# Compressed keys by four TensorE products over rows read back from memory, and later rows' statistics tied to program order

## The chip, the cores and the metric

One core of a Trainium2 chip runs the whole program: one launch, float32 throughout apart from small index products. The metric is device time in microseconds (us) of that core, the median of a few executions. Smaller is better. Engines are named as in the profile: PE is TensorE (matrix products and transposes), DVE is VectorE, ACT is ScalarE, POOL is GpSimd, SP is SyncE, which here only issues DMAs. PE writes to PSUM banks, which DVE or ACT must read out before a bank can be written again.

## The reference

Two transformer layers on four sequences of 512 tokens, 512 wide. Each layer adds an attention and a mixture of experts to its input. The part that matters here is the first layer's attention on the layer-normed rows `xn`. Besides a local window it attends to compressed entries, each a softmax-weighted sum of 4 neighbouring tokens:

```python
w_log = (hidden_states @ Wcmp + bcmp).reshape(Bq, C, RATIO)      # C = 128 entries, RATIO = 4
w_cmp = jax.nn.softmax(w_log, axis=-1)
entries = jnp.einsum('bcr,bcrh->bch', w_cmp, hidden_states.reshape(Bq, C, RATIO, HID))
ck = apply_rope(rmsnorm(entries @ Wk + bk, kn_w), block_ends)
cv = entries @ Wv + bv
sc = jnp.einsum('bhsd,bcd->bhsc', q, ck) * scale                 # scores against entries, top 8 kept
```

## The kernel before

**Rows and steps.** The 2048 tokens are 16 row tiles of 128 (n = 0..15), four to a sequence b. The first layer's attention has 16 heads in 8 groups g of two; a step is one pair (g, b), and there are 32, in the order of `steps` (g outer, b inner). Each step computes scores, context and output of its own pair and, in between, the projections of the next step (`project`: seven block products p1 to p7, each of two chunks and two contraction halves, line 661). Everything this change touches lies before step 4, in the first tenth of the run: row statistics, compression, and steps 0 to 3.

**Row tiles.** `layernorm(n)` (line 215) takes the statistics on DVE (`bn_stats` 221, aggregate 223, add 224), the inverse root on POOL (225, 227), the normed row `xn` (DVE for the first four tiles, ACT at 234 for the others: that is what `scaled` means), stores it to `xnd` in device memory (237), transposes it on PE (242) and copies the transpose into `xnT` on ACT (243). `start_sequence(n)` does all of it for one tile. Tiles 4 to 7 are called between the parts of the first projection, ahead of the loop; 8 to 11 in step 0 and 12 to 15 in step 1, one at each of the places (i, 0) to (i, 3) of `run0`.

**Logits and compression.** `first_logits(b)` computes the compression and router logits of a sequence from its four transposed tiles (252: four products of 32 columns of weights against 512 columns, then 259 to turn them back). `compress(b)` is a generator of four parts; for b = 0 they run ahead of the loop, for b = 1, 2, 3 at places 0, 1, 3.5 and 4 of step b - 1. Part 1 turns the logits (584) and takes the softmax on DVE and ACT (586 to 593); then four DVE operations spread each of the four weight columns over an identity (596). Part 2 lets one PE product with a matrix of ones put all 512 weights on every partition (`wB`, 599), and for each of the four chunks of 128 features DVE multiplies the transposed rows by them (603) and sums groups of four (604). Part 3 projects the entries (`kv`, 609), adds biases (611, 613), and norms and rotates `ck` (564 to 566, 573 to 576, 616). Part 4 transposes `ck` (619) into `ckT` (620), which the scores of step b need at line 744.

**Order.** The code's order is not the order on the engines: a scheduler of the tile framework places the instructions of all engines when the program is built, by its own estimates, and each engine then runs its list in order. `tc.keep_in_program_order(x)` ties an instruction to its place in the code, behind what the code issues on that engine before it. Before, this is done in `layernorm` only for the first four tiles, so that statistics of later tiles may move ahead. DVE's temporaries of `layernorm` are in a pool of three buffers, which limits how far ahead.

**PSUM.** Eight banks: three for projections and outputs ("mm"), three for scores, context, logits, `wB` and `kv` ("sc"), two for transposes ("tr"). A tag's banks are taken in turn.

## Time and profile before

| | us |
|---|---|
| median of 3 executions | 2073.09 (2073.08 to 2075.61) |
| the profiled execution's own time | 2074.66 |
| its span in the profile | 2072.6 |
| first score product of step 0 starts (line 744) | 61.44 |
| of step 1 | 102.89 |
| of step 2 | 149.12 |
| of step 3 | 193.31 |

Times in the profile are from the span's start. The step starts frame the stage the change is in: steps 0, 1 and 2 take 41.5, 46.2 and 44.2 us. In the profile's lines `L661` is a line of the kernel, an arrow points from a tile's operand to its result, `x4` counts instructions of the machine, and a bracket gives the idle time before an instruction and the engine that ended it. One float32 product of the code is two such PE instructions, so one block product and chunk of `project` is four of 384 columns (1.29 us where they run one behind the other) and a transpose of 128 by 128 is one.

### The profile page before, as it was taken

Reading aid. Unit: us, or ns where it says so; the run is one execution under the profiler, and the core shown is the slowest. Engines: PE = TensorE matmul, PEld = TensorE weight load, DVE = VectorE, ACT = ScalarE, POOL = GpSimd, SP = SyncE. Lnnn points to the kernel's source line nnn. Section 1 sums busy time; section 2 is a strip of 40 time slices with the busy share of each in tenths; the row PEclk is TensorE's granted clock in tenths of the full one; section 3 lists DMA queues with packets and bytes.
Section 4 is the critical chain, followed back from the end, with each engine's and each line's share of the span. In section 5 each row is a group of like instructions: output and inputs, shape, how many; then the busy total and the mean of one; then the engine's idle time right before and its main releaser. Section 6 shows DMA issues by size and latency. Waiting matters only on the chain.

```text
span 2072.6 us, 27984 instructions
## 1 busy us (share of the span) xinstructions
PE 2017.7 (97%) x9130; PEld 1205.3 (58%) x9130; DVE 1452.0 (70%) x3543; ACT 867.9 (42%) x2600; POOL 754.3 (36%) x761
## 2 busy tenths in 40 slices
PE   6999999999999999999999999999999999999997
PEld 4666666666666666666666666666334445445442
DVE  7888967666766666676667778787596555557775
ACT  4554444444444443444444455454243432333332
POOL 4422244443423333344333444353114332332550
PEclk9999999999999999999999999999999999999999
DMA  7102133333333343234443222121317765773551
GB/s 250 68 31 62 42 118 120 143 108 103 130 130 104 109 155 103 92 135 166 183 170 116 70 76 85 42 72 62 119 51 244 263 243 196 257 243 123 158 163 52
DMA packets 98906, 267.23 MB, mean 129 GB/s; under 512 B 14400, under 2 KB 27840, under 8 KB 87488
## 3 DMA queue, kind: packets, MB, share of 16 engines
q0 software_dynamic: 27072, 148.91, 21.4%
q1 hardware_dynamic: 70528, 114.34, 16.4%
q10 hardware_dynamic: 1152, 2.10, 0.3%
q8 instruction: 75, 1.23, 0.2%
q14 instruction: 79, 0.65, 0.1%
HBM read 222.05 MB, written 42.73 MB: 128 GB/s over the span
## 4 chain that ended last, share of the span: by engine, by line
PE 81%; DVE 8%; ACT 3%; POOL 2%; DMA 2%; issue 1%; SPq 0%; ACTq 0%; POOLq 0%; DVEq 0%
PE p L661 23%; PE hp_r L518 12%; PE op L828 10%; PE st L753 4%; PE st L1224 3%; PE qp L1200 3%; PE sp L744 3%; PE cx L1238 2%; PE ca L797 2%; PE o L1307 2%; PE trm_r L506 2%; PE vp L1160 1%; PE trq L681 1%; PE trk L687 1%; PE cc L800 1%
## 5 line engine op out<-in xcount | busy, mean ns | idle before, releaser
L828 PE MATMUL op<-Wo,cT 128*128 128x512 f32 x512 | 230.6, 598 | 5.3 <-DVE lv L725 2.9
L518 PE MATMUL hp_r<-we_r,xT_r 128*128 128x512 f32 (+1 forms) x592 | 224.8, 596 | 0.0
L470 POOL DMA_INDIRECT xr_r<-xnd,rows_r x72 | 89.4, 1242 | 331.6 <-PE trm_r L506 298.2
L761 POOL TENSOR_TENSOR lT<-lT,lmask 128x512 f32<-128x512 f32 (+1 forms) x128 | 157.6, 1244 | 140.8 <-ACT lT L757 140.6
L661 PE MATMUL p<-wT,x 128*128 128x384 f32 x512 | 179.6, 493 | 0.5 <-DVE wT L119 0.5
L661 PE MATMUL p<-wB,x 128*128 128x384 f32 x512 | 175.9, 488 | 4.0 <-DVE u L717 4.0
L661 PE MATMUL p<-wA,xnT 128*128 128x384 f32 x512 | 174.0, 492 | 0.2 <-DVE u L696 0.2
L828 PEld LDWEIGHTS op<-Wo,cT 128*128 128x128 f32 x512 | 92.0, 190 | 115.0 <-issue 77.2
L564 ACT ACTIVATE sq<-qb 128x128 f32<-128x128 f32 x384 | 118.9, 310 | 93.0 <-DVE qb L710 44.9
L1226 ACT ACTIVATE pT<-st 128x1024 f32<-128x1024 f32 x128 | 123.7, 1014 | 62.7 <-PE st L1224 57.0
L518 PEld LDWEIGHTS hp_r<-we_r,xT_r 128*128 128x128 f32 (+1 forms) x592 | 83.8, 170 | 97.3 <-issue 91.8
L831 DVE TENSOR_TENSOR acc<-acc,op 128x512 f32<-128x512 f32 x128 | 87.4, 685 | 69.4 <-PE op L828 69.0
L661 PEld LDWEIGHTS p<-wB,x 128*128 128x128 f32 x512 | 93.9, 190 | 68.5 <-issue 10.2
L661 PEld LDWEIGHTS p<-wT,x 128*128 128x128 f32 x512 | 94.5, 193 | 63.5 <-issue 6.7
L661 PEld LDWEIGHTS p<-wA,xnT 128*128 128x128 f32 x512 | 95.6, 193 | 61.0 <-issue 2.9
L675 ACT ACTIVATE qb<-qb,ss 128x128 f32<-128x128 f32 x256 | 81.9, 390 | 110.7 <-POOL ss L566 108.6
L508 ACT COPY xT_r<-trm_r 128x512 f32<-128x512 f32 x72 | 41.8, 581 | 198.0 <-PE hp_r L518 188.3
L757 ACT ACTIVATE lT<-st,ss 128x256 f32<-128x256 f32 (+1 forms) x128 | 47.2, 449 | 175.4 <-PE st L753 175.3
L753 PE MATMUL st<-qkT 128*128 128x256 f32 (+1 forms) x512 | 110.4, 357 | 0.0
L534 POOL DMA_INDIRECT row_r<-yd,slot_r x64 | 74.2, 1160 | 94.0 <-DVE row_r L1341 35.8
L753 PEld LDWEIGHTS st<-qkT 128*128 128x128 f32 x512 | 93.1, 193 | 11.4 <-issue 1.4
L566 POOL TENSOR_TENSOR ss<-ss,nhalf 128x6 f32<-128x6 f32 x64 | 95.7, 1496 | 5.3
(360 smaller groups left out, 4334.2 us busy)
## 6 DMA issues: line engine op xcount, KB each, us to landing
x<-xsd SPq DMA_DIRECT2D x112, 256.0 KB, 3.1
yd<-yr_r SPq DMA_DIRECT2D x72, 256.0 KB, 3.4
wA<-in_wA SPq DMA_DIRECT2D x16, 384.0 KB, 3.6
wB<-in_wB SPq DMA_DIRECT2D x16, 384.0 KB, 7.6
xnd<-xn SPq DMA_DIRECT2D x24, 256.0 KB, 2.0
accd<-acc SPq DMA_DIRECT2D x18, 256.0 KB, 2.0
acc<-in_x SPq DMA_DIRECT2D x16, 256.0 KB, 4.9
Wo<-in_Wo SPq DMA_DIRECT2D x8, 512.0 KB, 3.6
```

What stands on the lines that cost most here:

```text
L470: G.indirect_dma_start(out=out, out_offset=None, in_=src, in_offset=at_rows(idx))
L518: PE.matmul(hp[ts(h, m), :], lhsT=xT[:, k, ts(h, m)], rhs=w[:, ts(k, HID)], start=(k == 0), stop=(k == KC - 1))
L534: G.indirect_dma_start(out=x, out_offset=None, in_=self.yd, in_offset=at_rows(self.r.slot[:, k, n : n + 1]))
L564: A.activation(sq, x[:, h, :], AF.Square, accum_out=ss[:, h : h + 1])
L566: G.tensor_tensor(ss, ss, nhalf[:, 0:n], ALU.pow)
L661: PE.matmul(p, lhsT=x[:, k, ts(c, P)], rhs=w[:, k, :], start=(k == 0), stop=(k == 1))
L675: A.activation(x[:, j, :], x[:, j, :], AF.Copy, scale=sq[t][:, j : j + 1])
L753: PE.matmul(st[:, ds((t % 2) * 256, n)], lhsT=qkT[:, HG + h, ts(t, P)], rhs=qkT[:, h, ds(t * P, n)], start=True, stop=True)
L761: G.tensor_tensor(dst, dst, lmask.rearrange("p a w j -> p (a w j)")[:, 0:n], ALU.mult)
L828: PE.matmul(op, lhsT=cT[:, h, ts(t, P)], rhs=wo[:, h, :], start=(h == 0), stop=(h == HG - 1))
L831: V.tensor_tensor(acc[:, n, :], acc[:, n, :], op, ALU.add)
L1226: A.activation(pt[:, ts(pair, 2), :], st, AF.Exp, scale=SCALE1)
```

## The change

Line numbers on the minus side are those of the profile. In `compress`, the rows of a sequence are read back from `xnd` in one DMA of 1 MB at the start of part 1, queued on SP. A matrix `fold` (the sum of the identity's four blocks of 32 columns, so that fold[p, j] = 1 where p modulo 32 is j) is made once on POOL. DVE scales 32 columns instead of 128 by each weight column; PE transposes the result and ACT copies it (`wsel`); four products, each with 32 columns of `wsel` as weights and one row tile of 512 features as the moving side, give all 128 entries in one bank; ACT copies them, four transposes turn them, and ACT copies them into `entT`. From `kv` on nothing is different. The multiplications and sums at 603 and 604, and `wB`, are gone. In `layernorm`, tiles 4 to 15 of the first layer's sequence are now tied to program order as the first four were, and in `scores` the first DVE operation of head 0 is tied in steps with i < 2.

```diff
--- before.py
+++ after.py
@@ -175,8 +175,13 @@
 
     ident = const.tile([P, P], F32, tag="ident", name="ident")
     make_identity(nc, ident)
+
+    fold = sp0.tile([P, FEW], F32, tag="fold", name="fold", bufs=1)
     nhalf = const.tile([P, 8], F32, tag="nhalf", name="nhalf")
     G.memset(nhalf, -0.5)
+    G.tensor_tensor(fold, ident[:, ts(0, FEW)], ident[:, ts(1, FEW)], ALU.add)
+    for n in (2, 3):
+        G.tensor_tensor(fold, fold, ident[:, ts(n, FEW)], ALU.add)
     A.activation(small.tile([P, 8], F32, tag="warm", name="warm", bufs=1), nhalf, AF.Exp)
     ones_sq = const.tile([P, P], F32, tag="ones_sq", name="ones_sq")
     G.memset(ones_sq, 1.0)
@@ -216,7 +221,7 @@
 
 
 
-        pin = tc.keep_in_program_order if n < TC else (lambda x: x)
+        pin = tc.keep_in_program_order if n < TC or scaled else (lambda x: x)
         st = small.tile([P, 6], F32, tag="st", name=f"st_{n}")
         pin(V.bn_stats(st, acc[:, n, :]))
         mv = small.tile([P, 2], F32, tag="mv", name=f"mv_{n}")
@@ -578,6 +583,8 @@
     def compress(b, pool):
 
         w_row = row_w[b]
+        rows_ = pool.tile([P, TC, HID], F32, tag="rows4", name=f"rows4_{b}", bufs=1)
+        nc.sync.dma_start(out=rows_, in_=xnd[ts(b, S), :].rearrange("(n p) h -> p n h", p=P))
 
         wt = psum("tr", f"wt_{b}")
         for r in range(RATIO):
@@ -591,17 +598,26 @@
         A.activation(w1, w1, AF.Exp, bias=mx, accum_out=sm)
         V.reciprocal(sm, sm)
         V.tensor_scalar(w1, w1, sm, None, ALU.mult)
-        wd = pool.tile([P, C, RATIO], F32, tag="prod", name=f"wd_{b}", bufs=1)
+
+        wd = pool.tile([P, FEW, RATIO], F32, tag="wd", name=f"wd_{b}", bufs=1)
         for r in range(RATIO):
-            V.tensor_scalar(wd[:, :, r], ident, w1[:, r : r + 1], None, ALU.mult)
+            V.tensor_scalar(wd[:, :, r], fold, w1[:, r : r + 1], None, ALU.mult)
         yield
-        wB = psum("sc", f"wB_{b}")
-        PE.matmul(wB, lhsT=ones_sq, rhs=wd.rearrange("p c r -> p (c r)"), start=True, stop=True)
+        tr = psum("tr", f"trw_{b}")
+        PE.transpose(tr[:, 0:P], wd.rearrange("p c r -> p (c r)"), ident)
+        wsel = pool.tile([P, P], F32, tag="wd", name=f"wsel_{b}", bufs=1)
+        A.copy(wsel, tr[:, 0:P])
+
+        ep = psum("sc", f"ent_{b}")
+        for n in range(TC):
+            PE.matmul(ep[ts(n, FEW), :], lhsT=wsel[:, ts(n, FEW)], rhs=rows_[:, n, :], start=True, stop=True)
+        ent = pool.tile([P, HID], F32, tag="lr", name=f"ent_{b}", bufs=1)
+        A.copy(ent, ep)
+        tr = psum("tr", f"tre_{b}")
+        for k in range(KC):
+            PE.transpose(tr[:, ts(k, C)], ent[:, ts(k, P)], ident)
         entT = pool.tile([P, KC, C], F32, tag="entT", name=f"entT_{b}", bufs=1)
-        for k in range(KC):
-            prod = pool.tile([P, C, RATIO], F32, tag="prod", name=f"prod_{b}_{k}", bufs=1)
-            V.tensor_tensor(prod.rearrange("p c r -> p (c r)"), xnT[:, k, ts(b, S)], wB, ALU.mult)
-            V.tensor_reduce(entT[:, k, :], prod, AX.X, ALU.add)
+        A.copy(entT, tr.rearrange("p (k c) -> p k c", k=KC))
         yield
         kv = psum("sc", f"kv_{b}")
         for i, w in enumerate((wk, wv)):
@@ -744,7 +760,9 @@
             PE.matmul(sp[:, seen[t]], lhsT=qkT[:, h, ts(t, P)], rhs=ckT[:, b, 0 : 32 * (t + 1)],
                       start=True, stop=True)
         s = wk0.tile([P, SEEN[TC - 1].stop], F32, tag="s", name=f"s_{nm}")
-        V.tensor_tensor(s, sp[:, 0 : SEEN[TC - 1].stop], cmask, ALU.add)
+        s_ = V.tensor_tensor(s, sp[:, 0 : SEEN[TC - 1].stop], cmask, ALU.add)
+        if i < B - 2 and h == 0:
+            tc.keep_in_program_order(s_)
         lT = wk0.tile([P, TC * 2 * P - P], F32, tag="lT", name=f"lT_{nm}")
         for half in range(2):
             st = psum("sc", f"st{half}_{nm}")
```

The built program's order of instructions differs up to step 3 on PE, DVE, ACT, POOL and SP, and nowhere behind it.

## The prediction

> **What bounds it now.** First the page's busy times, then the stage in windows cut at the last product of each step's output (columns: busy us and instructions of PE, weight loads, DVE, ACT, POOL; granted PE clock; DMA share; GB/s).

> ```profile
> PE 2017.7 (97%) x9130; PEld 1205.3 (58%) x9130; DVE 1452.0 (70%) x3543; ACT 867.9 (42%) x2600; POOL 754.3 (36%) x761
> 55.00:101.90 46.90, 45.38 (x227) 31.91 (x225) 40.09 (x129) 25.38 (x85) 19.30 (x28) 0.96 0.19 69
> 101.90:148.15 46.25, 45.23 (x234) 31.14 (x234) 38.02 (x106) 24.21 (x81) 12.18 (x13) 1.00 0.10 35
> 148.15:192.90 44.75, 43.50 (x216) 29.65 (x216) 38.32 (x107) 20.96 (x76) 11.27 (x13) 1.00 0.22 69
> ```

> PE is full everywhere, in steps 0 to 2 too, where DVE is some 84% busy. So DVE time is worth only the PE idle time that it causes. I get that by adding up what PE has to do, with durations from the chain of waits (start, us, what):

> ```profile
> 60.65 0.33 PE trck L619
> 60.98 0.44 PE trg_r L259 x4
> 61.44 1.25 PE sp L744 x8
> 62.69 2.99 PE st L753 x8
> ...
> 68.69 1.52 PE st L753 x8
> ...
> 70.53 0.44 PE trx L242 x4
> 70.97 0.65 PE p L661 x2
> 71.62 0.86 PE wB L599 x2
> ...
> 101.97 0.99 PE lg_r L252 x8
> ```

> A block product is 4 x 0.32 = 1.29 us, four transposes 0.44, scores 1.09, `kv` 1.76 (16 x 0.11), an output 6.87. Later steps with two experts are 45.8 us apart; less 2 x 3.9 for the experts, 38.0 is a dense step. Sequence work comes on top. Step 1 (102.89 to 149.12) needs 38.0 + 1.8 (row transposes) + 1.0 + 0.4 + 0.4 (logits) + 0.9 (`wB`) + 1.8 + 0.1 = 44.4 of its 46.2: 1.8 lost. Step 2 needs 41.7 of 44.2: 2.5 lost, half of it waiting for `wd` (596). Step 0 needs 39.2 of 41.5, and 1.5 of its loss is the slow `st` above. From 41.04 to 61.44, ahead of step 0, PE needs 16.2 of 20.4: 4.2 lost. All that any relief can give back is 4.2 + 2.3 + 1.8 + 2.5 = 10.8 us.

> **What is removed and added.** Per sequence DVE loses eight operations (603, 604) and most of four:

> ```profile
> 46.61 0.67 DVE L603 TENSOR_TENSOR prod<-xnT,wB 128x512 f32<-128x512 f32 x1
> 47.67 0.67 DVE L604 TENSOR_REDUCE entT<-prod 128x128 f32<-128x512 f32 x1
> ```

> 8 x 0.67 = 5.4, and some 0.5 of the 0.9 to 2.0 that `wd` takes at a quarter of the width: 6 us each, 24 in all. PE loses `wB` (0.86) and gets five transposes (0.55) and four 32-column products like the logits' (0.99): +0.7 each, which lies on the bound engine. ACT gets copies of 128 and twice 512 columns (0.3 + 2 x 0.58): on an engine 45 to 55% busy their length is hidden, but they stand in its queue between PE and its next product. `fold` (three small POOL operations) runs before POOL's first use at 4.69, idle time. SP gets four 1 MB reads. Other 1 MB loads land in 5.4 to 10.1 us; rows 0 to 3 are stored long before, and the read is queued behind the fourth `xsd` store at some 41, so it lands by 46.5 to 51, and PE wants it at 49.9: hidden, or 1 us late. Later ones have more room; what is queued behind them on SP (`wB`, `xsd`) is wanted a step later.

> **What moves.** This decides. Before, statistics of tiles 6 and 7 ran on DVE at 40 to 41, and those of 8 to 11 by 43, far ahead of PE. Tied down, they stand behind what the code issues earlier, and in the new list of PE the transposes `trx` of a tile stand ahead of work that is ready. I merged the new lists by hand, each engine in order, with the durations shown. From statistics to transpose it is:

> ```profile
> 41.04 0.69 DVE L221 BATCH_NORM_STATS2 st<-acc 128x6 f32<-128x512 f32 x1
> 40.09 0.55 POOL L225 TENSOR_TENSOR mv<-mv,nhalf 128x1 f32<-128x1 f32 x1 [1.36 <-DVE mv L223]
> 40.74 0.27 POOL L227 TENSOR_SCALAR mv<-mv 128x1 f32<-128x1 f32 x1
> 43.87 0.80 ACT L234 ACTIVATE xn<-acc,mv 128x512 f32<-128x512 f32 x1
> ```

> *Ahead of step 0.* PE is dense from 41.4 on: eight block products 10.3, the new ones and `trq`, `trx` 2.4, `kv` 1.8, so `kv` ends at 55.9 (57.9 before). Only then can DVE add the biases and rotate `ck`, and behind these tile 7's statistics are tied: 0.5 + 1.0 (two `qb`) + 0.7 + 0.65 + other work in between 1.05 = 3.9, POOL 0.9, ACT 0.8: its `trx` starts at 61.6. PE has 0.44 to do meanwhile (`trk`) and idles 5.2. The copy to `xnT` stands behind two `qb` scalings that wait for a 1.34 us power on POOL: ready at 63.7; logits 1.0; scores start at 64.7 instead of 61.44: **+3.3**, its own share of the added PE work included. Bounds: +1.5 if DVE's in-between work is done earlier, +4.5 if the fetch is late too.

> *Step 0.* Tile 8's statistics follow the spread weights, whose softmax follows head 0's scores: DVE reaches them at 75.9, `trx` can start at 78.3, PE is there at 75.8 with the ready `trs` behind it: 2.5 lost. `wsel` waits in ACT's queue for `xn`, `xnT` and `s`: 0.7. Tile 11 costs about 1.0, and the 0.7 lost before is regained at best: with the 0.7 of PE work, 2.5 + 0.7 + 1.0 - 0.7 + 0.7 = 4.2; as `trs` no longer waits later I take **+3.5**. Bounds 0 (PE so late that rows are ready) and +6.

> *Step 1.* The list puts six block products ahead of tile 12's `trx`. The statistics of 12 and 13 delay the reading of the third (0.7 lost on the bank), `trx` 1.3, `wsel` 0.9, tile 14 0.8, the context's banks 0.7: 4.4 new, 1.8 old gone, 0.7 work: **+3.3**. Bounds -1.1 and +5.

> *Step 2* has no tiles: up to all of 2.5 regained, 0.7 paid: -1.8 to +0.7. By my merge the second context starts 0.3 earlier; I take **-0.5**.

> Sum 3.3 + 3.5 + 3.3 - 0.5 = 9.6. From step 3 on nothing is reordered, and PE is 97% busy, so the shift reaches the end whole. The span becomes 2082.2, and that execution 2084.3 by the 2.06 around its span; on the median of 2073.09 it is **2082.7**.

> [...] The row first (windows; PE busy, then clock):

> ```profile
> 58.00:60.00 2.00, 1.18 (x4) 0.38 (x2) 2.00 (x9) 0.50 (x3) 0.81 (x2) 1.00 0.39 139
> 60.00:62.00 2.00, 1.32 (x10) 1.09 (x11) 2.00 (x6) 1.55 (x8) 0.24 (x1) 1.00 0.34 131
> 62.00:64.00 2.00, 2.00 (x9) 1.73 (x9) 1.54 (x11) 0.21 (x1) 1.92 (x3) 0.59 0.35 131
> ```

> After four us at 60% busy, the clock is 0.59 and `st` takes 2.99 instead of 1.52. I put the same loss into both programs. [...]

> **Rivals.** *A, faster.* DVE's 24 us are what PE's losses come from; DVE runs ahead again, tied rows included, and PE never meets a `trx` too early. For it: before, DVE's chain carries `wd` into `wB` (1.0 and 1.2 idle). Against it: tiles 6 to 15 give up a lead of 10 us or more. Half of the 10.8 us won, and three quarters of the 2.7 of PE work paid, is -3.4; all and all paid, -8.1. It lies between 2065.0 and 2069.7, say 2068. It decides if step 0's scores start before 61.

> *B, no change.* The first gap is as I say (+3.3), but in steps 0 to 2 new waits only replace the old: 2.0 of PE work, -4.3 for the losses of steps 1 and 2, some +1: 2073.1 + 3.3 + 2.0 - 4.3 + 1.0 = 2075.

> *C, slower by the fetch.* SP holds a read until the last of its four tiles is stored (row stores land in 2.0), and tiles are now late; each of the four `ent` waits some 2 us more: 9.6 + 4 x 2 gives 2090. Against it: 2 to 20 us of room for all but the first.

> **Numbers.** Forecast (2077.3 to 2087) 0.58, C and worse 0.08, B 0.18, A 0.16. Since 0.2% (4.1 us, about what can be told from no change here) parts the signs, slower takes the forecast and C, 0.66; same is B, 0.18; faster is A, 0.16. Sum of the lower bounds 1.5 + 0 - 1.1 - 1.8 = -1.4, of the upper +16.2 (2089). Below stands A with 0.16, of which I leave half out: 2068 to 2089.

> **What would show it.** Right: `sp` of step 0 starts near 64.7 behind a PE gap of 4 to 6 us that tile 7's `xn` ends; `trx` waits of 1 to 3 us for `xn` (line 239 of the new code) in steps 0 and 1; DVE some 24 us less busy up to 195. Wrong: no PE wait on `xn` behind 45, or waits on the fetched rows, or step 3's scores starting before 193.

## The result, and the profile after

| | before | changed |
|---|---|---|
| median, us | 2073.51 (2073.08 to 2075.61, 4 runs) | 2093.53 (2092.06 to 2094.98, 4 runs) |
| ratio | | 1.0094, 95% interval 1.0082 to 1.0107 |
| the profiled execution: its own time / its span | 2074.66 / 2072.6 | 2092.06 / 2090.3 |

The changed kernel is slower, by 20.0 us on the medians, where 9.6 were forecast. The two profiled executions are 17.4 apart, because that of before lay 1.2 above its median and that of the changed kernel 1.5 below. What the traces can explain is 17.7 us of span. The starts of the steps' scores say where they arise:

| first score product of | before | changed | later by | forecast |
|---|---|---|---|---|
| step 0 | 61.44 | 65.15 | 3.71 | 3.3 |
| step 1 | 102.89 | 116.83 | 13.94 | 6.8 |
| step 2 | 149.12 | 166.51 | 17.39 | 10.1 |
| step 3 | 193.31 | 211.02 | 17.71 | 9.6 |
| step 4 | 224.88 | 242.60 | 17.72 | 9.6 |

From step 4 to step 23 the difference stays at 17.71 to 17.72. So step 0 grew by 10.2 us where 3.5 were forecast, and everything else came within 0.9.

The first lines of the changed kernel's page answer to those shown before, with the busy times of all engines:

```profile
PE 2024.3 (97%) x9174; PEld 1206.1 (58%) x9174; DVE 1435.2 (69%) x3511; ACT 874.4 (42%) x2612; POOL 755.3 (36%) x764
```

DVE has 16.8 us less to do (24 were forecast), PE is busy for 6.6 longer. The same columns as in the windows of the prediction (busy us and instructions of PE, weight loads, DVE, ACT, POOL; granted PE clock; DMA share; GB/s), first from the end of the first projection to step 0's scores and then step by step, and below that some stretches of 2 us:

```profile
55.80:65.15 9.35, 2.92 (x15) 0.81 (x14) 5.68 (x17) 6.50 (x23) 3.48 (x6) 0.79 0.12 43
65.15:116.83 51.68, 45.93 (x228) 31.52 (x225) 31.27 (x102) 23.56 (x70) 14.71 (x20) 0.91 0.29 101
116.83:166.51 49.68, 47.14 (x245) 30.89 (x241) 34.54 (x109) 26.62 (x86) 16.21 (x21) 1.00 0.18 61
166.51:211.02 44.51, 43.67 (x225) 30.08 (x221) 33.59 (x98) 22.62 (x78) 12.09 (x13) 1.00 0.24 74
...
64.00:66.00 2.00, 2.00 (x12) 0.85 (x5) 1.25 (x2) 0.66 (x2) 0.58 (x1) 0.50 0.60 223
72.00:74.00 2.00, 2.00 (x15) 1.88 (x15) 1.76 (x6) 0.56 (x2) 0.97 (x2) 1.00 0.05 12
82.00:84.00 2.00, 2.00 (x6) 0.93 (x4) 0.65 (x2) 1.23 (x5) 0.00 (x0) 0.50 0.21 77
```

PE is idle for 5.8 of the 51.7 us of step 0, where before it was idle for none, and its clock averages 0.91 there against 0.96. DVE, busy for 86% of step 0 before, is at 61%: the engine that was relieved is not the one that PE waits for. The waits of PE between 41 and 215 us name what it waits for (us in total, times, longest):

```profile
PE trx L247 <- ACT xn L239: 12.6, 7, 4.9
PE lg_r L257 <- ACT xnT L248: 1.5, 1, 1.5
PE trw L607 <- DVE wd L604: 0.8, 1, 0.8
```

It is the normed rows, seven times, and never the fetched rows: `ent` of sequence 0 starts at 49.12 with no wait. PE's list around step 0 shows the two long waits (start, us, what; in brackets the idle time and who ended it):

```profile
55.26 0.60 PE L703 MATMUL trk<-ident,qb 128*128 128x128 f32 x4
60.76 0.79 PE L247 MATMUL trx<-ident,xn 128*128 128x128 f32 x4 [4.90 <-ACT xn L239]
...
63.28 1.94 PE L257 MATMUL lg_r<-xnT,wr 128*32 128x512 f32 x8 [1.53 <-ACT xnT L248]
65.15 2.08 PE L760 MATMUL sp<-ckT,qkT 128*128 128x32 f32 x8
...
74.45 3.39 PE L677 MATMUL p<-wT,x 128*128 128x384 f32 x10
80.91 0.65 PE L247 MATMUL trx<-ident,xn 128*128 128x128 f32 x4 [3.07 <-ACT xn L239]
...
81.81 1.49 PE L677 MATMUL p<-wT,x 128*128 128x384 f32 x2
```

Read the durations too. Scores take 2.08 here and 1.06 a few us later, a pair of 384-column products 1.49 instead of 0.81: after each of the two long gaps the clock is at 0.50, from 61.1 to 71.4 and from 81.6 to 85.0.

Why tile 8's statistics are late is seen in DVE's list, with what POOL does at that time:

```profile
75.40 2.50 DVE L604 TENSOR_SCALAR wd<-fold,w 128x32 f32<-128x32 f32 x4
77.81 0.68 DVE L226 BATCH_NORM_STATS2 st<-acc 128x6 f32<-128x512 f32 x1
...
75.44 2.26 POOL L779 TENSOR_TENSOR lT<-lT,lmask 128x512 f32<-128x512 f32 x2 [2.47 <-ACT lT L775]
```

The statistics stand behind the spread weights, as forecast, and these four operations of 32 columns take 2.50 us beside two POOL operations, where the median of all sixteen is 0.24 each. So the quarter width saved nothing at the place that counts. That POOL is what stretches them is only read from the overlap; no run took it apart.

### The profile page after: what moved, and what is told of

The parts are those of the page before. It is cut to its first block, busy times and chain, and to the rows that moved or that the text cites. A ratio compares the mean times of both kernels' runs of the same rounds, so it can differ in the third digit from the quotient of the medians.

```text
span 2090.3 us, 28075 instructions
## 1 busy us (share of the span) xinstructions
PE 2024.3 (97%) x9174; PEld 1206.1 (58%) x9174; DVE 1435.2 (69%) x3511; ACT 874.4 (42%) x2612; POOL 755.3 (36%) x764
## 3 DMA queue, kind: packets, MB, share of 16 engines
q8 instruction: 76, 1.25, 0.2%
## 4 chain that ended last, share of the span: by engine, by line
PE 76%; DVE 9%; ACT 3%; POOL 2%; issue 2%; DMA 1%; ACTq 0%; DVEq 0%; POOLq 0%
PE p L677 22%; PE hp_r L523 12%; PE op L846 10%; PE st L771 4%; PE st L1242 3%; PE qp L1218 3%; PE sp L760 2%; PE cx L1256 2%; PE o L1325 2%; PE ca L815 2%; PE trm_r L511 2%; PE vp L1178 1%; PE trq L697 1%; PE cb L818 1%; PE ca L813 1%
## 5 line engine op out<-in xcount | busy, mean ns | idle before, releaser
L569 ACT ACTIVATE sq<-qb 128x128 f32<-128x128 f32 x384 | 118.8, 309 | 85.3 <-DVE qb L726 41.7
L849 DVE TENSOR_TENSOR acc<-acc,op 128x512 f32<-128x512 f32 x128 | 87.6, 685 | 71.5 <-PE op L846 71.1
L677 PEld LDWEIGHTS p<-wT,x 128*128 128x128 f32 x512 | 94.9, 194 | 63.5 <-issue 5.8
```

What stands on the lines that cost most here:

```text
L569: A.activation(sq, x[:, h, :], AF.Square, accum_out=ss[:, h : h + 1])
L677: PE.matmul(p, lhsT=x[:, k, ts(c, P)], rhs=w[:, k, :], start=(k == 0), stop=(k == 1))
L849: V.tensor_tensor(acc[:, n, :], acc[:, n, :], op, ALU.add)
```

## The experiments

All profiles in one table. The four columns of steps say how much later than in the kernel before each step's first score product starts, in the profiled execution; the last columns are medians and ratios to the runs of before on the same chip (medians 2073.5 to 2074.0). A start also moves when PE's list puts work on the other side of it; the start of step 3, behind which nothing is reordered, is free of that.

| kernel | step 0 | step 1 | step 2 | step 3 | median, us | ratio, 95% interval |
|---|---|---|---|---|---|---|
| changed | 3.71 | 13.94 | 17.39 | 17.71 | 2093.53 | 1.0094 (1.0082 to 1.0107) |
| comp_alone | -0.22 | 3.08 | 3.80 | 4.12 | 2079.60 | 1.0028 (1.0017 to 1.0040) |
| ties_alone | 6.19 | 13.15 | 18.56 | 18.01 | 2091.77 | 1.0092 (1.0076 to 1.0107) |
| free_4_to_7 | -2.74 | 5.55 | 9.01 | 9.35 | 2086.13 | 1.0060 (1.0046 to 1.0074) |
| tie_4_to_7 | 3.78 | 9.63 | 10.36 | 10.68 | 2085.38 | 1.0064 (1.0050 to 1.0078) |
| no_score_tie | 7.44 | 15.30 | 18.74 | 19.06 | 2096.17 | 1.0110 (1.0095 to 1.0126) |
| filled_gap | 3.08 | 10.91 | 14.36 | 14.68 | 2091.90 | 1.0089 (1.0075 to 1.0102) |
| dve_relief | -5.29 | -2.67 | -2.37 | -1.56 | 2074.48 | 1.0001 (0.9992 to 1.0010) |
| comp_late_part2 | -1.60 | -1.09 | 0.09 | -0.47 | 2076.05 | 1.0011 (1.0001 to 1.0020) |
| comp_wd_on_act | -1.75 | 0.72 | 1.97 | 2.41 | 2078.81 | 1.0025 (1.0014 to 1.0037) |
| before_filled5 | -3.07 | -4.05 | -4.07 | -4.05 | 2070.51 | 0.9987 (0.9977 to 0.9996) |
| before_filled6 | -0.33 | -1.44 | -1.46 | -1.48 | 2072.73 | 0.9997 (0.9988 to 1.0006) |
| comp_late_filled5 | -4.87 | -4.36 | -3.16 | -3.72 | 2073.02 | 1.0004 (0.9995 to 1.0013) |

### The two halves of the change

The compression without the ties:

```diff
-        pin = tc.keep_in_program_order if n < TC or scaled else (lambda x: x)
+        pin = tc.keep_in_program_order if n < TC else (lambda x: x)
...
-        if i < B - 2 and h == 0:
-            tc.keep_in_program_order(s_)
```

> The new compression with all three ties undone (layernorm of tiles 4 to 15 and the score's first DVE operation). Theory P (the ties: statistics stand late in DVE's list and PE's transposes wait for them): no wait of PE on xn above 0.5 us behind 45 us, step 0's scores start at 57 to 60, step 3's before 193.3, time 2066 to 2076 against 2073.5 before. Theory F (the fetched rows and the chain trw, wsel, ent, tre hold PE up): step 3's scores start at 203 or later and the time is 2083 or more, with waits on wsel, ent or entT.

The old compression with the ties (the same lines, put into the kernel before):

> The old compression (wB, multiplications and sums on DVE) with all three ties. Theory P: PE waits for xn of tiles 7, 8 and others as in the changed kernel, and DVE has 24 us more to do in the same stretch: 2088 to 2100. Theory F: without the fetch and its chain little is lost, 2073 to 2082.

Both cost time by themselves. The ties alone give 2091.77, nearly the whole loss, with waits for `xn` as in the changed kernel (8.1 us in nine places). The compression alone waits for no `xn` above 0.5 us, starts step 0 at 61.22 (57 to 60 was expected) and yet costs 4.1 us by step 3 and 5.6 on the median, between what the two theories said: 2079.60 is neither 2066 to 2076 nor 2083. Three lines of its PE list, all in step 0, say where:

```profile
69.11 0.55 PE L795 MATMUL trs<-ident,s 128*128 128x128 f32 x3 [0.90 <-ACT s L786]
73.31 0.30 PE L607 MATMUL trw<-ident,wd 128*128 128x128 f32 x1 [1.72 <-DVE wd L604]
93.18 1.56 PE L677 MATMUL p<-wB,x 128*128 128x384 f32 x4 [1.11 <-DVE u L733]
```

3.7 us of waits, in a step that had none before (against them, the dip of the clock that the kernel before has in this step, worth 1.7 us, is missing here). Less work on DVE did not make `wd` earlier; the new PE list asks for it when it is not there.

The two halves do not add up: 4.1 and 18.0 us alone by step 3, 17.7 together. On top of the ties the compression costs nothing more, so how much of the 17.7 is its own depends on the order in which one takes the change apart.

### Which ties

Tiles 4 to 7 untied, and then tiles 8 to 15 untied:

```diff
-        pin = tc.keep_in_program_order if n < TC or scaled else (lambda x: x)
+        pin = tc.keep_in_program_order if n < TC or n >= 2 * TC and scaled else (lambda x: x)
```

```diff
-        pin = tc.keep_in_program_order if n < TC or scaled else (lambda x: x)
+        pin = tc.keep_in_program_order if n < 2 * TC and (n < TC or scaled) else (lambda x: x)
```

> The changed kernel with tiles 4 to 7 untied, tiles 8 to 15 tied. Theory P: the 4.9 us gap ahead of tile 7's transposes goes and step 0's scores start by 60; with the gap goes the halved clock that followed it to 71.5 (some 3 us); the 3.1 us gap at tile 8 stays: 2083 to 2088. Theory F: the changed kernel's 2093 stays.

> The new compression with the ties of tiles 4 to 7 and of the scores, tiles 8 to 15 untied. If the two groups of ties cost independently, step 3's scores start 8.1 us (17.7 less 9.6) behind those of the new compression alone, at some 205.5, and the time is 2086 to 2089. If tiles 8 to 15 only catch up what 4 to 7 delayed, it is 2090 or more; if the other way round, under 2084.

Untying 4 to 7 took the 4.9 us gap away, as expected; tile 8's grew to 4.15, and 2086.13 is inside the range. With only 4 to 7 tied, step 3 starts at 203.99 (some 205.5 expected) and the median, 2085.38, lies between the first and the last branch: nearly independent, not quite. Over the compression alone, 4 to 7 cost 6.6 us of span, and 8 to 15 cost 5.2; with the compression's 4.1 that is 15.9 of the 17.7, so 1.8 us come only with both groups. Both kernels keep the tie on the scores, so each of the two shares contains what that tie costs.

The tie of the scores' first operation removed:

```diff
-        if i < B - 2 and h == 0:
-            tc.keep_in_program_order(s_)
```

> The changed kernel without the tie on the scores' first DVE operation; statistics of tiles 4 to 15 stay tied. If the score's tie adds to the lateness of tile 8, its wait shrinks from 3.1 to under 2 us, no halved clock follows it, and the time is 2087 to 2091. If the statistics' tie alone does it, the wait stays near 3 us and the time 2092 to 2095.

Inconclusive. Tile 8's wait fell to 1.99, no halved clock followed, and step 0 took 49.31 instead of 51.68, as the first branch says. But this kernel reached step 0 at 68.88, 3.7 later than the changed one, mostly through PE's wait ahead of 29.22 (8.49 us instead of 6.12), in a stretch whose order is the same in both; the median, 2096.17, is above both branches. That wait ends with rows scaled by a power that POOL computes, and POOL is late long before that. Its first addition of biases here, and the same in the changed kernel:

```profile
16.09 1.00 POOL L120 TENSOR_TENSOR b<-b 128x384 f32<-128x384 f32 x1 [2.39 <-DMA bcmp<-in_bcmp]
```

```profile
14.13 1.00 POOL L120 TENSOR_TENSOR b<-b 128x384 f32<-128x384 f32 x1 [1.25 <-DMA wcol<-in_kn_w]
```

The power starts at 26.69 here and at 24.45 there. So the loads at the start of the run, by the profile, made this kernel late there, and not the order of its work; why they came later is open. From step 0's start to step 1's it is 2.4 us faster than the changed one, of which the missing dip is 1.7.

### The gap and the clock

Five products put into the 4.9 us gap:

```diff
         def turn():
             xn, tr = made["xn"], bank("tr", f"trx_{n}")
+            for _ in range({7: 5}.get(n, 0) if scaled else 0):
+                pin(PE.matmul(tr, lhsT=ident, rhs=xnT[:, 0, 0:HID], start=True, stop=True))
```

> The changed kernel with five products of 128x512 (some 4.3 us, result unused) put into PE's list just ahead of tile 7's transposes, where PE is idle for 4.9 us; all other lists but for three places of ACT's are the same. If the gap is what halves the granted clock from 61 to 71.5, the clock there is 1.00, step 0's scores start up to 1 us earlier and the step is 3 us shorter: 2088 to 2091. If the clock drops for another reason, it stays 0.5 there and the time is 2093 to 2095.

PE's list of this kernel, where the changed one has its gap (the first line is the filling):

```profile
56.23 4.46 PE L247 MATMUL trx<-xnT,ident 128*128 128x512 f32 x10
61.28 0.66 PE L249 MATMUL trx<-ident,xn 128*128 128x128 f32 x4 [0.60 <-ACT xn L239]
...
64.52 1.16 PE L762 MATMUL sp<-ckT,qkT 128*128 128x32 f32 x8
...
66.38 1.25 PE L773 MATMUL st<-qkT 128*128 128x256 f32 x6
```

The scores take 1.16 instead of 2.08 and `st` 1.25 instead of 2.34, and the clock is 1.00 from 63.5 to 76.5, where the changed kernel has 0.50 up to 71.4. Rows arrive no earlier, and 4.3 us of useless work makes the span 3.0 shorter at step 3: 0.6 ahead of step 0 and 2.4 in it. The median fell by 1.6, to just above the expected range, its runs (2089.65 to 2092.22) reaching into it. The halved clock is the gap's doing.

### What DVE's time is worth

```diff
-            prod = pool.tile([P, C, RATIO], F32, tag="prod", name=f"prod_{b}_{k}", bufs=1)
-            V.tensor_tensor(prod.rearrange("p c r -> p (c r)"), xnT[:, k, ts(b, S)], wB, ALU.mult)
-            V.tensor_reduce(entT[:, k, :], prod, AX.X, ALU.add)
+            A.copy(entT[:, k, :], wB[:, ts(k, C)])
```

> The kernel before with the four multiplications and four sums per sequence left out on DVE: ACT copies 128 columns of wB into entT four times in their place (compressed entries are then not the reference's). PE's work is unchanged, DVE has some 21 us less to do. Theory P (DVE time is worth only the PE idle time that it causes, 4.3 us at most in steps 1 and 2 and up to 4 ahead of step 0): 2067 to 2074. Rival A of the prediction (DVE is where PE's losses come from): 2062 to 2067.

Nothing: 1.0001. With 32 DVE operations of 0.68 us left out of the kernel before, step 0 starts 5.3 earlier, and 3.7 of that are given back by step 3; the median is the same. Most of the 5.3 is no gain: PE's list has 12 instructions of products (3.9 us) behind step 0's first scores that it had ahead of them before. And the 1.6 us that remain at step 3 are about what the kernel before loses to the dip of its clock behind 62 us (1.7); here the clock is 1.00 from 41 to 215 us. This is what the change set out to remove, at no cost in PE work, and it is worth nothing that the median shows.

### What is left of the compression

Its second part called one place later, so that PE comes to `trw` after the first head's context:

```diff
-        for t in (0, 1, 3.5, 4):
+        for t in (0, 2, 3.5, 4):
```

> The new compression without ties, its second part (trw, wsel, ent, tre, entT) called at place 2 of a step instead of place 1, so that PE's list has trw behind the row products and not ahead of them. If the 5.5 us that the compression costs by itself are the waits for wd (2.5 us) and what stands behind them, 2073 to 2077. If it is PE's added work and the ACT copies, 2078 to 2081.

The waits on `wd` are gone. Step 3 starts 4.6 earlier than with the compression alone, and 0.5 earlier than before, though PE has more to do than before (it is spared the dip of 1.7 us, too); the median, 2076.05, is in the first branch, but still 2.2 above that of before. Next, the compression without ties again, its second part back at place 1, with `wd` scaled on ACT:

```diff
-            V.tensor_scalar(wd[:, :, r], fold, w1[:, r : r + 1], None, ALU.mult)
+            A.activation(wd[:, :, r], fold, AF.Copy, scale=w1[:, r : r + 1])
```

> The new compression without ties, the four spread weights (wd) scaled on ACT instead of DVE. If the waits for wd come from DVE's queue and its stalls beside POOL (four operations took 2.5 us in the changed kernel's step 0), they go and the time is 2075 to 2078. If wd waits for the softmax before it, 2079 to 2081.

It removes less: 1.7 us of span and 0.8 of the median, which falls between the branches, and `trw` now waits for ACT, 2.7 us in three places. The place in PE's list was the larger cost, not the engine.

### A version faster than both

If a gap of 5 us costs what was shown, so does the 6.1 us wait ahead of 27 us that the kernel before has as well. Five products there:

```diff
     first_logits(0)
+    fill = psum("tr", "fill")
+    for _ in range(5):
+        tc.keep_in_program_order(PE.matmul(fill, lhsT=ident, rhs=xnT[:, 0, 0:HID], start=True, stop=True))
     second(0)
```

> The kernel before with five products of 128x512 (4.3 us, result unused) in the 6.1 us in which PE is idle from 21.1 to 27.2, ahead of step 0. If the gap is what halves the clock there from 25 to 35, the clock stays 1.00, PE's work from 27.2 to 35 takes 4 us instead of 8, and the step starts move 2 to 4 us earlier: 2069 to 2072 against 2073.8. If PE waits for weights or DVE there anyway, 2072 to 2075.

> As before_filled5 with six products (5.2 us), which leaves 0.9 us idle; the order of the first products behind them changes a little. 2069 to 2073 if the clock theory holds, 2073 to 2076 if not.

> The new compression without ties, its second part at place 2, and the same five products in PE's idle time at 21 us. Clock theory: 2 to 4 us below the 2076.05 of the same kernel without them, 2072 to 2074; step 3's scores start by 190.5.

Windows of the kernel before, and then of the one with five products:

```profile
30.00:32.00 2.00, 2.00 (x4) 1.09 (x4) 1.73 (x7) 0.39 (x2) 0.62 (x2) 0.50 0.36 134
32.00:34.00 2.00, 2.00 (x4) 1.08 (x4) 1.28 (x4) 0.81 (x1) 0.20 (x1) 0.50 0.03 10
```

```profile
30.00:32.00 2.00, 2.00 (x8) 1.21 (x7) 1.97 (x8) 0.90 (x2) 1.18 (x4) 1.00 0.58 216
32.00:34.00 2.00, 2.00 (x7) 1.15 (x7) 1.22 (x6) 1.11 (x3) 0.82 (x2) 1.00 0.55 207
```

Fifteen products instead of eight in the same time. The steps move 4.05 us earlier and the median is 2070.51, 0.9987 of before with an interval that ends at 0.9996: the fastest kernel of this study, if by little, without any part of the change. Six products change the order behind them and keep only 1.5 us of it (2072.73, in the first range). The compression with its second part late and the same filling starts step 3 at 189.59, 3.7 ahead of before, as expected; its median of 2073.02 is not told apart from before.

## Why the prediction was wrong

The direction and the mechanism were right, and so was the first gap almost line by line: 5.2 us of idle PE forecast and 4.90 measured, scores at 64.7 forecast and 65.15 measured. Step 1 (3.3, measured 3.45) and step 2 (-0.5, measured 0.32) hold too. The step that failed is "I take **+3.5**" for step 0, which measured 10.2. Its parts, the kernel before having no wait of PE in that step:

- Waits. Forecast were 2.5 (`trx` of tile 8), 0.7 (`wsel`) and 1.0 (tile 11), less 0.7 regained: 3.5. Measured were 3.07 (tile 8), 1.22 (tile 10) and 1.44 (tile 11): 5.7, so 2.2 too little. `wsel` cost nothing that shows as a wait of PE. Neither the 0.7 to be regained nor the 0.7 by which the text then went from 4.2 to 3.5, for `trs`, was there to win: before, PE is idle for 0.02 us in the whole step.
- Clock. "I put the same loss into both programs." Step 0 loses 0.09 x 51.68 = 4.7 us to the clock, and before it lost 0.04 x 41.45 = 1.7: 3.0 forecast at nothing. The text had looked at one 1.48 us gap with a dip behind it and took the dip for the same after a gap three times as long, and its sum has nothing for the clock behind the later gaps. Measured are 10.2 us at half clock behind the first gap, 6.2 of them in step 0, and 3.4 behind the second, against 3.4 in the kernel before. *filled_gap* shows the larger part of it: without the first gap step 0 is 2.4 us shorter.
- The remaining 10.2 - 5.7 - 3.0 = 1.5 stand against 0.7 of PE work. Of the other 0.8, 0.4 are the four transposes `trg_r`, which PE's list had ahead of step 0's scores before (60.98) and has behind them now (67.87); the rest is not settled.

The 10.8 us that the prediction called lost before, as all that relief could give back, were too many. From 41 us to step 3 PE is idle for 4.2: 1.9 ahead of step 0, none in it, 1.0 and 1.3 in steps 1 and 2; the dip costs another 1.7.

Of what is removed and added: the 24 us of DVE were 16.8. Operations that follow each other overlap in the trace (one starts at 47.67 before the one ahead of it, 0.54 from 47.21, has ended), so 0.67 each was too much: *dve_relief*, which leaves out the same 32, has 16.3 less. And `wd` saved next to nothing, 4.9 us before and 4.7 after. The reads were hidden, as forecast; rival C's waits do not exist. Rival A fell with *dve_relief*: its premise, that DVE's load causes PE's losses, does not hold for the kernel before. Rival B's 4.3 us for the losses of steps 1 and 2 did not come back either. The prediction put nearly all of the loss on the moved statistics, and *ties_alone* bears it out (18.0 by step 3); what it did not see is that the compression's own list costs 4.1 where the ties are absent.

## What to carry to other kernels

Where one engine is 97% busy, as PE is here, an operation taken off another one is worth only the waits that it causes (16.3 us of DVE were worth nothing that the median shows, *dve_relief*), and a list that asks for a value earlier loses what the faster producer won (3.7 us of waits in step 0 of *comp_alone*): look at when the bound engine comes to it. A tie to program order is paid where the code issues much work ahead of the tied operation (18.0 us by step 3, *ties_alone*). And a gap in PE's list costs its length and can cost more: behind gaps of 1.48 to 6.13 us PE ran at a clock of 0.50 for 3.4 to 13.7 us in these profiles, though not behind each (see below). Where the gap can't be closed, useless products in it can pay (step 3 starts 3.0 us earlier in *filled_gap*, 4.05 in *before_filled5*).

## What the hardware showed unasked

| gap, us | where | clock behind it |
|---|---|---|
| 0.9 to 1.25 (many), 1.41 to 2.12 (several) | all kernels | 1.00 |
| 1.48 | before, ahead of step 0 | 0.50 for 3.4 us, from 1.7 us behind it |
| 1.48 | before_filled5, the same place | 1.00 |
| 3.04 | before_filled5, 27.71 | 1.00 |
| 3.07, 3.69, 4.15 | changed, filled_gap, free_4_to_7, tile 8 | 0.50 for 3.4 us, from 0.7 to 1.1 us behind it |
| 3.26, with 0.90 and 0.89 shortly before it | ties_alone, 63.98 | 0.50 for 10.2 us, from its end on |
| 4.90 | changed, tile 7 | 0.50 for 10.2 us, from 0.4 us behind it |
| 4.89, 4.90 | tie_4_to_7, no_score_tie, tile 7 | 0.50 for 13.7 us, from within it |
| 6.13 | before, 27.19 | 0.50 for 10.2 us, from within it |

Four lines of the list of before_filled5, with the filling, the gap of 3.04 and that of 1.48:

```profile
20.21 4.46 PE L1005 MATMUL fill<-xnT,ident 128*128 128x512 f32 x10
27.71 0.33 PE L681 MATMUL trq<-ident,qb 128*128 128x128 f32 x1 [3.04 <-ACT qb L675]
...
54.64 1.46 PE L661 MATMUL p<-wA,xnT 128*128 128x384 f32 x4
57.58 0.33 PE L619 MATMUL trck<-ident,ck 128*128 128x128 f32 x1 [1.48 <-ACT ck L616]
```

The same wait of 1.48 us was followed by a dip in one kernel and by none in the other, 3 us earlier in time; step 0 takes 40.47 us there instead of 41.45, which is 1.0 of the 4.05 won. The share of time in which PE is busy around the wait does not tell the two apart either. Windows of the kernel before up to its dip and in it (its clock changes at 62.38 and 65.79), of before_filled5 around the same wait, and of the changed kernel up to its second dip and in it (first PE's busy time, then the clock in the third column from the right):

```profile
58.96:62.38 3.42, 1.92 (x14) 1.47 (x14) 3.31 (x12) 1.64 (x8) 1.35 (x3) 1.00 0.39 143
62.38:65.79 3.41, 3.41 (x12) 2.87 (x12) 3.06 (x19) 1.56 (x5) 3.01 (x3) 0.50 0.20 77
...
56.00:58.00 2.00, 0.52 (x5) 0.42 (x5) 2.00 (x9) 1.04 (x6) 0.67 (x2) 1.00 0.60 218
58.00:60.00 2.00, 1.98 (x15) 1.67 (x13) 1.63 (x5) 0.60 (x3) 1.23 (x2) 1.00 0.33 127
60.00:62.00 2.00, 2.00 (x17) 1.91 (x15) 2.00 (x19) 1.29 (x4) 1.92 (x2) 1.00 0.01 4
...
78.21:81.62 3.41, 0.71 (x7) 0.71 (x7) 3.38 (x13) 0.83 (x2) 0.80 (x2) 1.00 0.00 0
81.62:85.04 3.42, 3.42 (x12) 1.51 (x14) 0.92 (x4) 1.61 (x5) 0.68 (x2) 0.50 0.20 77
```

Before, PE is busy for 1.92 of the 3.42 us up to the dip, 56%; the dip starts 1.73 us behind the wait. In before_filled5 the 3.42 us that end 1.73 behind the wait, 55.89 to 59.31, hold 1.9 us of PE as well by its list and these windows, and the clock stays at 1.00 up to 66. Ahead of the second dip of the changed kernel PE was busy for 0.71 of 3.41 us, 21%. What decides whether a dip follows is not shown: no run here moved a gap alone.

Behind step 31 the kernels differ again, though nothing is reordered there: from the last step's first scores to the end they take 646.80 us (ties_alone) to 650.45 us (comp_late_part2), 648.08 before. In the last 160 us PE is idle for 16.0 in both the kernel before and the changed one, and the granted clock falls to 0.50 there, for 3.4 us from 1973.7 on before and for 6.8 us from 2054.5 on in the changed kernel. Differences of 2 us between medians are therefore not read as effects of the edit here; the steps' starts, whose differences stay within 0.04 us from step 4 to step 23, are.
